# SmoothQuant woven further into the table lookups, and the softplus of the state-space scan in pairs of groups

## The chip, the core and the metric

The kernel runs on one core of one Trainium2 chip. The metric is the device time of one execution in microseconds. Three runs of the kernel before took 1949.47, 1953.06 and 1958.2 us; the median, 1953.06 us, is what the changed kernel is compared with.

## The reference, cut to what matters

The program is a stack of four residual blocks on x of shape (4 batches, 512 positions, 512 channels):

```python
x = x + smooth_quant_mlp(layernorm(x), fside, ctx)     # per batch; int8-like quantization
x = x + ghost_ffn(layernorm(x), lut, gate_idx, up_idx, down_idx)   # weights are lut[idx]
x = x + mamba(ctx, layernorm(x), ...)                  # state-space scan, gated by x
x = x + moe(layernorm(x), gate_w, w_gate, w_up, w_down)            # 32 experts, top 8
```

In the third block the step size goes through a softplus before the scan over the 512 positions, with 16 states for each of 512 inner channels:

```python
u  = silu(conv(in_proj(ctx)) + conv_b)
dt_low, Bm, Cm = split(x_proj(u))
dt = softplus(dt_proj(dt_low) + dt_b)
state = state * exp(dt * A) + (dt * u) * B;   y = sum_n(state * C)
```

`ctx` is an input, so everything up to `dt` and `dt * u` depends on no earlier block; only the gate with layernorm(x) does. The quantized multiplication scales both operands by column maxima, rounds each row to 127 steps of its own maximum, multiplies, and scales back.

## The kernel before, in words

The program is written as Python generators, each of which yields after a step. `weave` (L1053) takes several generators with a weight each and always advances the one that has done the smallest share of its weight. A scheduler then puts the emitted instructions into one queue for each engine; every engine works through its own queue in order. Pools hand out memory: when a pool is closed and another opened, the new tiles wait for the last use of what lay there.

**Lookups** (`lut_weights`, L317). The FFN's weights are built in 27 jobs of four steps. In a step VectorE compares the indices with a value (L335, `oh`, one-hot rows in bf16), TensorE multiplies them with the table in three bf16 parts (L341, `pw`), and ScalarE copies the result out (L350).

**SmoothQuant** (`smooth_quant`, L196; `quantize`, L159). One generator of 26 steps for each batch; `staggered` starts the next batch 15 steps after the one before. In `quantize` VectorE scales the rows (L166) and takes their maxima (L171 to L173), ScalarE rounds (L176, L180), TensorE transposes and ScalarE copies (L186, L187). It is called for x, for the weights w, for the intermediate a, and for the down weights `dw`. Outputs `o` are scaled on VectorE (L247) and added to x on GpSimd (L248). The four batches have 104 steps. In the kernel before, 40 of these are woven with the first 48 lookup steps, 48 with the rest (L1080 to L1082), and what is left with `prepare` of batch 0 (L1088).

**prepare** (L482), nine steps for each batch: for each of four groups of 128 channels a projection (`pi`), the convolution on VectorE (L496 to L505); then `px`, `xd`, and the softplus of each of the four groups (L519 to L537). The softplus is max(z, 0) + log(1 + exp(-|z|)), with the rounding of 1 + w put right by `lost`: Abs, Relu and Exp on ScalarE (L526 to L528), one operation on VectorE (L530), a subtraction on GpSimd (L531), Ln on ScalarE (L532), two additions and the product with u on GpSimd (L533 to L535), and the store of `dt` and `dt * u` to memory (`dts`, L536, through GpSimd's queue). Exp and Ln change the activation table (`ACT_TABLE_LOAD` in the profile). The tile `d` of a group has two buffers, `lost` has one.

**Scan** (`scan`, L539): 64 rounds for each batch. Each loads `d` from `dts` with its rows repeated for the 16 states (L557, SyncE's queue), takes exp on ScalarE (L562, `st`), the product with B on GpSimd (L564, `dBu`, three buffers), the scan itself on VectorE (L567 or L569) and the product with C (L570 on VectorE, L574 on GpSimd); TensorE sums the states (L580).

The scan of batch b is woven with the FFN of all batches in turn (`lut_ffn`, L353: layernorm L112, transposes `pt_x` L367 and copy `xT` L368, `pgu` L376 on TensorE, `g` and `h` L384 to L386, `po_f` L392), with `prepare` of batch b + 1, and with gate and routing of batch b - 1. `prepare` of batch 0 has no such company: it runs with the end of SmoothQuant. After the last batch come the experts (L921 to L976).

Of the kernel before, what the change touches and what calls it, by code (L numbers as in the profile page):

```python
# [16 lines left out]
F32 = mybir.dt.float32  # L17
# [4 lines left out]
AF = mybir.ActivationFunctionType  # L22
ALU = mybir.AluOpType
# [4 lines left out]
P = 128  # L28
NB = 4
S = 512  # L30
# [3 lines left out]
KH = HID // P  # L34
# [6 lines left out]
RANK = 16  # L41
# [19 lines left out]
class Kernel:  # L61
# [420 lines left out]
    def prepare(self, mp, up, b):  # L482

        nc, t = self.nc, self.t
        conv_b, dt_b, _ = (self.vecs[:, i, :] for i in range(3))
        cT = mp.tile([P, DC // P, S], F32, tag="c", name="cT", bufs=1)
        nc.sync.dma_start(out=cT, in_=t["ctxT"][b].rearrange("(k p) l -> p k l", p=P))
        u = self.u[b] = up.tile([P, KH, S], F32, tag="u", name="u", bufs=1)
        for e in range(KH):
            pi = self.bank(self.prep_tag, "pi")  # L490
            for k in range(DC // P):
                nc.tensor.matmul(
                    pi, lhsT=self.in_w[:, k, e * P : (e + 1) * P], rhs=cT[:, k, :], start=k == 0, stop=k == DC // P - 1
                )
            acc = mp.tile([P, S], F32, tag="acc", name="acc", bufs=1)
            nc.scalar.activation(  # L496
                acc, pi, AF.Identity, bias=conv_b[:, e : e + 1], scale=self.conv_w[:, e, 3:4]
            )
            for j in (2, 1, 0):
                a = 3 - j  # L500
                nc.vector.scalar_tensor_tensor(
                    acc[:, a:], pi[:, : S - a], self.conv_w[:, e, j : j + 1], acc[:, a:], ALU.mult, ALU.add
                )
            nc.scalar.activation(u[:, e, :], acc, AF.Tanh)
            nc.vector.scalar_tensor_tensor(u[:, e, :], u[:, e, :], 1.0, acc, ALU.add, ALU.mult)  # L505
            yield

        px = self.bank(self.prep_tag, "px")
        nx = RANK + 2 * NST
        for e in range(KH):  # L510
            nc.tensor.matmul(px[:nx, :], lhsT=self.xp_w[:, e, :], rhs=u[:, e, :], start=e == 0, stop=e == KH - 1)
        xd = mp.tile([P, DC // P, S], F32, tag="c", name="xd", bufs=1)[:nx, 0, :]
        nc.scalar.copy(xd, px[:nx, :])
        nc.scalar.dma_start(out=self.xdbl[b].rearrange("g n l -> (g n) l"), in_=xd)
        yield

        for e in range(KH):  # L519
            pd = self.bank(self.prep_tag, "pd")  # L520
            nc.tensor.matmul(
                pd, lhsT=self.dt_w[:, e * P : (e + 1) * P], rhs=xd[:RANK, :], start=True, stop=True
            )
            d = mp.tile([P, 2, S], F32, tag="dt", name="dt", bufs=2)
            dt, w = d[:, 0, :], d[:, 1, :]
            nc.scalar.activation(w, pd, AF.Abs, bias=dt_b[:, e : e + 1])  # L526
            nc.scalar.activation(dt, pd, AF.Relu, bias=dt_b[:, e : e + 1])
            nc.scalar.activation(w, w, AF.Exp, scale=-1.0)  # L528
            lost = mp.tile([P, S], F32, tag="acc", name="lost", bufs=1)
            nc.vector.tensor_scalar(lost, w, 1.0, -1.0, ALU.add, ALU.add)  # L530
            nc.gpsimd.tensor_tensor(lost, w, lost, ALU.subtract)  # L531
            nc.scalar.activation(w, w, AF.Ln, bias=1.0)  # L532
            nc.gpsimd.tensor_tensor(dt, dt, lost, ALU.add)  # L533
            nc.gpsimd.tensor_tensor(dt, dt, w, ALU.add)
            nc.gpsimd.tensor_tensor(w, dt, u[:, e, :], ALU.mult)  # L535
            nc.gpsimd.dma_start(out=self.dts[b, e * P : (e + 1) * P], in_=d)  # L536
            yield  # L537

    def scan(self, mp, b):  # L539

# [494 lines left out]
def run(steps):  # L1035
    for _ in steps:
        pass
# [25 lines left out]
@with_exitstack  # L1063
def tile_kernel(ctx: ExitStack, tc: tile.TileContext, t: dict):
    k = Kernel(tc, t)
    k.constants(ctx)
    scan = ExitStack()
    with ExitStack() as early:
        with ExitStack() as ffn:
            wp = ffn.enter_context(tc.tile_pool(name="wp", bufs=1, side="right"))  # L1070
            with ExitStack() as first:
                k.banks(first, t=2, m=2, y=2, d=2)
                ap = first.enter_context(tc.tile_pool(name="ap", bufs=2))
                sq = staggered([k.smooth_quant(ap, b) for b in range(NB)], 15)
                with ExitStack() as lut:
                    lc = lut.enter_context(tc.tile_pool(name="lc", bufs=1, side="right"))
                    lp = lut.enter_context(tc.tile_pool(name="lp", bufs=2, side="right"))
                    k.lut_tables(lc, wp)
                    lookups = k.lut_weights(lp, k.jobs)
                    weave((islice(sq, 40), 40), (islice(lookups, 48), 48))  # L1080
                    k.tile_rows(wp, lc)
                    weave((islice(sq, 48), 48), (lookups, 4 * len(k.jobs) - 48), (k.scratch(lc), 18))  # L1082

                pp = ffn.enter_context(tc.tile_pool(name="pp", bufs=1, side="right"))
                k.scan_weights(pp)
                k.prep_tag = "y"
                preps = 2 * KH + 1
                weave((k.prepare(pp, pp, 0), preps), (sq, 30 * NB - 88))  # L1088
            k.banks(early, t=2, m=2, y=1, d=3)
            k.prep_tag = "t"  # L1090
            bp = ffn.enter_context(tc.tile_pool(name="bp", bufs=2, side="right"))
            rp = ctx.enter_context(tc.tile_pool(name="rp", bufs=1))
            mp = scan.enter_context(tc.tile_pool(name="mp", bufs=2))
            k.routing_constants(rp)
            steps = (TPB // 2) * (NIC + 3)
            units = KH * 16
            routes = 2 * (TPB + 1)

            ffn_ = chain(*(k.lut_ffn(bp, b) for b in range(NB)))
            run(islice(ffn_, 4))  # L1100
            for b in range(NB):
                n = steps
                streams = [(k.scan(mp, b), units), (islice(ffn_, n), n)]
                if b + 1 < NB:
                    streams.append((k.prepare(pp, (pp, mp)[(b + 1) % 2], b + 1), preps))
                if b:
                    run(k.gate(mp, b - 1))
                    streams.append((k.route(rp, b - 1), routes))
                if b == NB - 1:
                    tok = k.slots(rp, k.tables[:1], 0, EARLY, ROOM[0], "a")  # L1110
                    at = k.slot_tokens(rp, tok, ROOM[0], "a")
                weave(*streams)
        ep = ctx.enter_context(tc.tile_pool(name="ep", bufs=2, side="right"))
        k.gu_tag = "m"
        full, nc = SLOTS // P, tc.nc
        two = [k.sums[j % 2] for j in range(full + 1)]
        first = k.pipeline(k.expert(ep, e, (k.xln[0], *at, 0), e, ROOM[0], two) for e in range(EARLY))
        weave((chain(k.gate(mp, NB - 1), k.route(rp, NB - 1)), KH + routes), (first, 2 * EARLY))
    scan.close()
    k.banks(ctx, t=4, g=4)  # L1120
    k.gu_tag = "g"
    tp = ctx.enter_context(tc.tile_pool(name="tp", bufs=6))
    at = k.slot_tokens(rp, k.slots(rp, k.tables, EARLY, NE, SLOTS, "u"), SLOTS, "u")
    at_b = k.slot_tokens(rp, k.slots(rp, k.tables[1:], 0, EARLY, ROOM[1], "b"), ROOM[1], "b")
    k.overflow(rp)
    calls = [(e, at, e - EARLY, SLOTS) for e in range(EARLY, NE)]
    for e in range(EARLY - LAST):
        calls.insert(2 * e + 1, (e, at_b, e, ROOM[1]))

    calls += [(e, at_b, e, ROOM[1]) for e in range(EARLY - LAST, EARLY)]  # L1130
    sums = [two] * (len(calls) - LAST) + [k.sums[2:] * 3] * LAST
    late = k.pipeline(
        k.expert(ep, e, (k.xln[1], *at, 0), col, n, s) for (e, at, col, n), s in zip(calls, sums)
    )
    run(islice(late, 2 * (len(calls) - LAST)))
    weave(
        (late, 2 * LAST),
        (
            chain(k.add_sums(tp, k.sums[:2], 0, NT // 2, True), k.add_sums(tp, k.sums[:2], NT // 2, NT, False)),
            NT // 2,  # L1140
        ),
    )
    run(k.add_sums(tp, k.sums[2:], NT // 2, NT, True))
    more = nc.values_load(k.more[0:1, 0:1], min_val=0, max_val=1)
    with tc.If(more):
        k.in_full(rp, ep, tp)
# [51 lines left out]
```

## Time and profile before

| | |
|---|---|
| median of three runs | 1953.06 us |
| the profiled execution | 1955.34 us |
| its span | 1953.5 us |
| granted TensorE clock, mean | 0.935 |
| TensorE busy | 1661.3 us (85%) |
| VectorE busy | 1196.9 us (61%) |
| GpSimd busy | 1001.9 us (51%) |
| ScalarE busy | 711.6 us (36%) |
| last lookup matmul | about 272.8 us |
| last addition of SmoothQuant (L248) | 340.4 us |
| first exponential of the scan (L562) | 350.7 us |
| first matmul of the FFN (L376) | 352.0 us |
| first expert gather (L902) | 1107.4 us |

How to read the profile: each line of the view in order of time has the start in us, the duration in us, the engine, the line of the kernel, the operation, output<-inputs by the program's names, the shape and the number of instructions merged into the line; in brackets stands how long the engine had been idle, and what it had waited for. PE is TensorE, PEld its weight loads, DVE is VectorE, ACT is ScalarE, POOL is GpSimd, SP is SyncE; a q behind the name is the engine's queue of DMA issues. The table of stretches has, for each stretch, the busy time of each engine in us with its number of instructions.

### The profile page before, as it was taken

Reading aid. Unit: us, or ns where it says so; the run is one execution under the profiler, and the core shown is the slowest. Engines: PE = TensorE matmul, PEld = TensorE weight load, DVE = VectorE, ACT = ScalarE, POOL = GpSimd, SP = SyncE. Lnnn points to the kernel's source line nnn. Section 1 sums busy time; section 2 is a strip of 40 time slices with the busy share of each in tenths; the row PEclk is TensorE's granted clock in tenths of the full one; section 3 lists DMA queues with packets and bytes.
Section 4 is the critical chain, followed back from the end, with each engine's and each line's share of the span. In section 5 each row is a group of like instructions: output and inputs, shape, how many; then the busy total and the mean of one; then the engine's idle time right before and its main releaser. Section 6 shows DMA issues by size and latency. Waiting matters only on the chain.

```text
span 1953.5 us, 25018 instructions
## 1 busy us (share of the span) xinstructions
PE 1661.3 (85%) x8836; PEld 983.6 (50%) x8845; DVE 1196.9 (61%) x2033; ACT 711.6 (36%) x1345; POOL 1001.9 (51%) x824
## 2 busy tenths in 40 slices
PE   4778875899889888898888588899999999999981
PEld 2444332656454545454545245455656656665640
DVE  6888864788799989998899734423222222232333
ACT  1554455545543554355333322222222222222210
POOL 3210113768755784578466642455555555555421
PEclk9989986899999898899899799999999999999995
DMA  9535611889887887778789696688887877778776
GB/s 264 142 104 165 203 60 35 224 200 226 213 236 162 200 218 201 172 195 207 192 209 221 175 226 140 152 195 177 184 181 157 178 180 169 164 166 191 148 163 210
DMA packets 190362, 351.94 MB, mean 180 GB/s; under 512 B 41826, under 2 KB 88258, under 8 KB 190228
## 3 DMA queue, kind: packets, MB, share of 16 engines
q1 hardware_dynamic: 147844, 253.00, 48.9%
q0 software_dynamic: 39952, 92.66, 24.0%
q10 hardware_dynamic: 2432, 4.59, 0.6%
q8 instruction: 72, 1.18, 0.3%
q14 instruction: 62, 0.51, 0.1%
HBM read 279.17 MB, written 79.47 MB: 184 GB/s over the span
## 4 chain that ended last, share of the span: by engine, by line
PE 35%; DMA 7%; DVE 5%; issue 2%; ACT 1%; POOL 1%; SPq 0%; ACTq 0%; POOLq 0%; DVEq 0%
PE pg L927 17%; PE po_e L956 8%; PE po_e L960 5%; PE pt_g L915 3%; DMA sums<-ey,to 2%; DMA xg<-xln,tokens 2%; DMA d<-dts 2%; DVE st L569 1%; DVE sc L570 1%; DMA acc<-sums 1%; POOL xg L902 0%; POOL dBu L564 0%; DVE lo_i L803 0%; PE pl L712 0%; DVE eh L945 0%
## 5 line engine op out<-in xcount | busy, mean ns | idle before, releaser
L970 POOL DMA_INDIRECT sums<-ey,to x168 | 261.3, 1555 | 314.1 <-DMA sums<-ey,to 129.8
L927 PE MATMUL pg<-exT,egu 128*128 128x320 f32 (+1 forms) x1536 | 402.7, 420 | 11.7 <-DVE exT L917 5.0
L564 POOL TENSOR_TENSOR dBu<-d,BC 128x512 f32<-128x512 f32 x256 | 333.9, 1315 | 107.8 <-DMA d<-dts 67.1
L927 PEld LDWEIGHTS pg<-exT,egu 128*128 128x128 f32 x1536 | 291.3, 192 | 126.4 <-issue 35.3
L569 DVE TENSOR_TENSOR_SCAN st<-st,dBu 128x512 f32<-128x512 f32 x192 | 230.8, 1216 | 32.1 <-POOL dBu L564 30.0
L562 ACT ACTIVATE st<-d,A 128x512 f32<-128x512 f32 x256 | 173.4, 689 | 202.1 <-DVE sc L570 125.8
L376 PE MATMUL pgu<-xT,wg 128*128 128x256 f32 (+1 forms) x704 | 189.4, 412 | 28.5 <-DVE h L386 23.5
L902 POOL DMA_INDIRECT xg<-xln,tokens x168 | 161.8, 963 | 90.5 <-PE pt_g L915 37.7
L944 DVE SCALAR_TENSOR_TENSOR eh<-eh,pg 64x128 f32<-64x128 f32 (+5 forms) x144 | 61.1, 425 | 223.5 <-ACT eh L943 222.4
L956 PE MATMUL po_e<-ed,eh 128*128 128x512 f32 (+1 forms) x336 | 171.5, 629 | 20.9 <-DVE eh L945 13.0
L376 PEld LDWEIGHTS pgu<-xT,wg 128*128 128x128 f32 (+1 forms) x704 | 133.5, 199 | 96.2 <-DVE h L386 34.6
L341 PE MATMUL pw<-oh,lut_t 128*32 128x344 bf16 (+1 forms) x2052 | 124.9, 356 | 65.6 <-DVE oh L335 65.3
L376 PE MATMUL pgu<-xT,wu 128*128 128x256 f32 (+1 forms) x704 | 176.8, 393 | 0.0
L969 ACT ACTIVATE ey<-po_e,gates 128x512 f32<-128x512 f32 (+1 forms) x104 | 68.7, 684 | 290.2 <-PE po_e L960 143.4
L967 DVE TENSOR_SCALAR ey<-po_e,gates 128x512 f32<-128x512 f32 x64 | 45.8, 747 | 201.3 <-PE po_e L960 201.3
L392 PE MATMUL po_f<-wd,h 128*128 128x512 f32 (+1 forms) x352 | 160.7, 613 | 2.9 <-DVE h L386 2.2
L376 PEld LDWEIGHTS pgu<-xT,wu 128*128 128x128 f32 (+1 forms) x704 | 136.2, 195 | 24.3 <-issue 3.0
L574 POOL TENSOR_TENSOR sc<-sc,BC 128x512 f32<-128x512 f32 x64 | 83.5, 1304 | 111.3 <-DVE sc L567 82.0
L570 DVE TENSOR_TENSOR sc<-st,BC 128x512 f32<-128x512 f32 x192 | 127.2, 678 | 17.9 <-PE py L580 17.3
L960 PE MATMUL po_e<-ed,eh 64*128 64x512 f32 (+1 forms) x336 | 112.8, 635 | 0.0
L341 PEld LDWEIGHTS <-lut_t 128*32 128x32 bf16 x2052 | 56.4, 101 | 111.9 <-issue 72.3
L392 PEld LDWEIGHTS po_f<-wd,h 128*128 128x128 f32 (+1 forms) x352 | 68.3, 197 | 87.3 <-issue 80.3
(259 smaller groups left out, 2194.1 us busy)
## 6 DMA issues: line engine op xcount, KB each, us to landing
d<-dts SPq DMA_DIRECT2D x256, 512.0 KB, 6.2
egu<-in_w_gate SPq DMA_DIRECT2D x40, 384.0 KB, 4.0
sums<-zero SPq DMA_DIRECT2D x16, 768.0 KB, 6.6
ix<-idx_b SPq DMA_DIRECT2D x16, 688.0 KB, 5.5
egu<-in_w_up SPq DMA_DIRECT2D x40, 256.0 KB, 5.6
ed<-in_w_down SPq DMA_DIRECT2D x40, 256.0 KB, 4.2
ed<-in_w_down SPq DMA_DIRECT2D x80, 128.0 KB, 4.3
acc<-sums SPq DMA_DIRECT2D x20, 512.0 KB, 9.1
```

What stands on the lines that cost most here:

```text
L341: nc.tensor.matmul(pt[i][32 * c : 32 * c + 32, :step], lhsT=self.lut_t[:, j, g, :], rhs=oh[:, c * n + i * step : c * n + (i + 1) * step], ...
L376: nc.tensor.matmul(pg[:m, j * W : (j + 1) * W], lhsT=w[:, k, c * P : c * P + m], rhs=xT[:, k, :], start=k == 0, stop=k == KH - 1,)
L392: nc.tensor.matmul(po, lhsT=h[:m, c, i * P : (i + 1) * P], rhs=self.wd[:m, c, :], start=c == 0, stop=c == NIC - 1,)
L562: nc.scalar.activation(st, d[:, 0, :], AF.Exp, scale=self.A[:, i : i + 1])
L564: product = nc.gpsimd.tensor_tensor(dBu, d[:, 1, :], BC[:, 0, :], ALU.mult)
L569: nc.vector.tensor_tensor_scan(st, st, dBu, 0.0, ALU.mult, ALU.add)
L570: nc.vector.tensor_tensor(sc, st, BC[:, 1, :], ALU.mult)
L902: nc.gpsimd.indirect_dma_start(out=xg[:m, :], out_offset=None, in_=xln, in_offset=bass.IndirectOffsetOnAxis(ap=tokens[:m, lo + j, col : co ...
L927: nc.tensor.matmul(pg[i][:, :hs], lhsT=w[:, k, i * P : (i + 1) * P], rhs=xT[:, k, z : z + hs], start=k == 0, stop=k == KH - 1,)
L956: nc.tensor.matmul(po[j][:m, :], lhsT=h[:, 0, b : b + m], rhs=wd[:, 0, :], start=True, stop=False)
L960: nc.tensor.matmul(po[j][:m, :], lhsT=h[r : r + R, 1, b : b + m], rhs=wd[r : r + R, 1, :], start=False, stop=True)
L970: nc.gpsimd.indirect_dma_start(out=sums[j], out_offset=bass.IndirectOffsetOnAxis(ap=to[:m, lo + j, col : col + 1], axis=0), in_=y[:m, :], ...
```

## The change

Two constants of the weave go up: 46 steps of SmoothQuant instead of 40 go with the first 48 lookup steps, 56 instead of 48 with the rest, so that 102 of the 104 steps are emitted beside the lookups and two beside `prepare` of batch 0. In `prepare` the softplus handles two groups at a time: the Abs and Relu of both, Exp of both, the `lost` part of both, Ln of both, then for each group the last addition, the product and the store. For batch 0 the subtraction, the additions and the product go to VectorE; for the other batches they stay on GpSimd. The buffers are as they were (two of `d`, one of `lost`). In the lines after it, the changed kernel's numbers are ten higher.

```diff
-        for e in range(KH):
-            pd = self.bank(self.prep_tag, "pd")
-            nc.tensor.matmul(
-                pd, lhsT=self.dt_w[:, e * P : (e + 1) * P], rhs=xd[:RANK, :], start=True, stop=True
-            )
-            d = mp.tile([P, 2, S], F32, tag="dt", name="dt", bufs=2)
-            dt, w = d[:, 0, :], d[:, 1, :]
-            nc.scalar.activation(w, pd, AF.Abs, bias=dt_b[:, e : e + 1])
-            nc.scalar.activation(dt, pd, AF.Relu, bias=dt_b[:, e : e + 1])
-            nc.scalar.activation(w, w, AF.Exp, scale=-1.0)
-            lost = mp.tile([P, S], F32, tag="acc", name="lost", bufs=1)
-            nc.vector.tensor_scalar(lost, w, 1.0, -1.0, ALU.add, ALU.add)
-            nc.gpsimd.tensor_tensor(lost, w, lost, ALU.subtract)
-            nc.scalar.activation(w, w, AF.Ln, bias=1.0)
-            nc.gpsimd.tensor_tensor(dt, dt, lost, ALU.add)
-            nc.gpsimd.tensor_tensor(dt, dt, w, ALU.add)
-            nc.gpsimd.tensor_tensor(w, dt, u[:, e, :], ALU.mult)
-            nc.gpsimd.dma_start(out=self.dts[b, e * P : (e + 1) * P], in_=d)
-            yield
+        tt = (nc.gpsimd if b else nc.vector).tensor_tensor
+        for e0 in range(0, KH, 2):
+            ds = []
+            for e in (e0, e0 + 1):
+                pd = self.bank(self.prep_tag, "pd")
+                nc.tensor.matmul(
+                    pd, lhsT=self.dt_w[:, e * P : (e + 1) * P], rhs=xd[:RANK, :], start=True, stop=True
+                )
+                d = mp.tile([P, 2, S], F32, tag="dt", name="dt", bufs=2)
+                nc.scalar.activation(d[:, 1, :], pd, AF.Abs, bias=dt_b[:, e : e + 1])
+                nc.scalar.activation(d[:, 0, :], pd, AF.Relu, bias=dt_b[:, e : e + 1])
+                ds.append(d)
+            for d in ds:
+                nc.scalar.activation(d[:, 1, :], d[:, 1, :], AF.Exp, scale=-1.0)
+            for d in ds:
+                dt, w = d[:, 0, :], d[:, 1, :]
+                lost = mp.tile([P, S], F32, tag="acc", name="lost", bufs=1)
+                nc.vector.tensor_scalar(lost, w, 1.0, -1.0, ALU.add, ALU.add)
+                tt(lost, w, lost, ALU.subtract)
+                tt(dt, dt, lost, ALU.add)
+            for d in ds:
+                nc.scalar.activation(d[:, 1, :], d[:, 1, :], AF.Ln, bias=1.0)
+            for e, d in zip((e0, e0 + 1), ds):
+                dt, w = d[:, 0, :], d[:, 1, :]
+                tt(dt, dt, w, ALU.add)
+                tt(w, dt, u[:, e, :], ALU.mult)
+                nc.gpsimd.dma_start(out=self.dts[b, e * P : (e + 1) * P], in_=d)
+                yield
...
-                    weave((islice(sq, 40), 40), (islice(lookups, 48), 48))
+                    weave((islice(sq, 46), 46), (islice(lookups, 48), 48))
                     k.tile_rows(wp, lc)
-                    weave((islice(sq, 48), 48), (lookups, 4 * len(k.jobs) - 48), (k.scratch(lc), 18))
+                    weave((islice(sq, 56), 56), (lookups, 4 * len(k.jobs) - 48), (k.scratch(lc), 18))
...
-                weave((k.prepare(pp, pp, 0), preps), (sq, 30 * NB - 88))
+                weave((k.prepare(pp, pp, 0), preps), (sq, 30 * NB - 102))
```

## The prediction

> **What bounds the kernel now.** I read the page first, then a table of stretches, then the order of time on each engine from 255 to 362 us, where both parts of the change meet. The page gives TensorE 85% of the span, but this is an average, so the table of stretches comes next (busy us and instructions per engine, then TensorE's clock, DMA share, GB/s):
>
> ```profile
> 0.00:273.00 273.00, 197.09 (x2599) 109.74 (x2607) 216.69 (x392) 118.18 (x187) 52.78 (x64) 0.94 0.54 164
> 273.00:341.00 68.00, 39.26 (x126) 17.57 (x127) 33.55 (x53) 38.20 (x57) 17.12 (x16) 0.71 0.13 42
> 352.00:1100.00 748.00, 658.68 (x3014) 402.12 (x3014) 666.23 (x1012) 335.47 (x545) 496.31 (x393) 0.94 0.82 203
> ```
>
> The lookups (0 to 273) are bound by VectorE: 216.7 of 273 us, and TensorE waits for its one-hot rows (65.3 us on the page's L341 row). The stretch 273 to 341 has no busy engine: nothing is over 58%. It is a chain of waits, the end of SmoothQuant's last batch woven with the first `prepare`. From 352 to 1100 (scan and FFN) VectorE is busy 89% and TensorE 88%; the experts after it are TensorE's. So a microsecond taken from the chain between 273 and 352 moves all later work forward, and one added to VectorE before 273 is paid in full.
>
> What ends that chain is seen in three answers. SyncE's queue, ScalarE, and TensorE with VectorE, in order of time:
>
> ```profile
> 340.44 0.37 SPq L622 DMA_DIRECT2D gate_w<-in_gate_w  x1
> 340.85 1.21 SPq L547 DMA_DIRECT2D BC<-xdbl  x2
> 342.17 16.35 SPq L557 DMA_DIRECT2D d<-dts  x7
> ```
> ```profile
> 340.45 0.81 ACT L112 ACTIVATE xn<-x,ln_off,ln_rs 128x512 f32<-128x512 f32 x1 [5.06 <-POOL x L248]
> ...
> 347.50 1.28 ACT L532 ACT_TABLE_LOAD   x1
> 348.80 0.63 ACT L532 ACTIVATE dt<-dt 128x512 f32<-128x512 f32 x1
> 349.45 1.28 ACT L562 ACT_TABLE_LOAD   x1
> 350.74 0.69 ACT L562 ACTIVATE st<-d,A 128x512 f32<-128x512 f32 x1
> ```
> ```profile
> 352.00 3.78 PE L376 MATMUL pgu<-xT,wg 128*128 128x256 f32 x8 [1.64 <-ACT xT L368]
> ```
> ```profile
> 352.01 1.22 DVE L567 TENSOR_TENSOR_SCAN sc<-st,dBu 128x512 f32<-128x512 f32 x1
> 356.79 2.45 DVE L569 TENSOR_TENSOR_SCAN st<-st,dBu 128x512 f32<-128x512 f32 x2 [3.56 <-POOL dBu L564]
> ```
>
> Everything new waits until 340.4, when GpSimd's last add of SmoothQuant (L248) frees the memory: the scan's loads (BC, d) and the FFN's `xn`. After that ScalarE still has two softplus groups with table loads before the first `st` at 350.74. VectorE's second scan waits to 356.8, because GpSimd is still at the fourth softplus.
>
> **SmoothQuant further beside the lookups.** The built order of the changed kernel shows what moves: ahead of the last one-hot row VectorE gets four instructions more, and only these, the scaling and row maximum of the last batch's weights (L166 2.29, L171 2.29, L172 0.17, L173 0.18: 4.9 us from their rows at 273.9 to 278.9). VectorE has little idle time there (1.96 us at 253.5 is the only long gap from 245 to 270), so the last one-hot row ends at 270.1 + 4.9 = 275.0. Bounds: 0 if gaps take them, 6 if earlier regrouping costs too; I take 4.9. The last lookup matmul follows 1.2 us later: 276.2, not 272.8 (before, its matmuls stood behind transposes; now these stand behind it). The load of `in_w` waits for it, so SyncE's seven small loads and `cT` (issued 272.9 to 276.3) move by 3.4 us and the first `pi` matmul from 280.5 to 284. Its cover: TensorE now has SmoothQuant's `q_w` transposes and `ph` to do in these 8 us; before it sat idle 6.65.
>
> SmoothQuant itself comes forward: the weights' row scale is known at about 273, not 278.9, so quantizing on ScalarE (2.93 + 2.00), transposes and copies bring the first `h` to 282.5 from 288.8. Behind it the order now favours SmoothQuant: all four `h` and the maximum of `a` stand ahead of the first convolution, and ScalarE has no softplus between `q_a`, `dw` and `q_d` (before: two Abs/Relu/Exp, one Ln, three loads at 1.28, 8.5 us, from 312.9 to 327), GpSimd none between its four adds. Walking the queues with the rows' durations: maximum of `a` 287.6, its scale 296.9, `q_a` 301, `dw` 307.5 to 311.4, `row_d` 317, four outputs with adds at 1.27 to 1.58: SmoothQuant ends at about 323, 17 us earlier. The walk has thirty hand-overs between engines, and a few tenths are easily missed in each: 323 to 330.
>
> `prepare` is not earlier: 3.5 us late at `pi`, four convolutions at 5.9 us each (from the starts of L496: 284.3, 290.3, 296.0, 302.0), `px`, `xd`: the first Abs at about 315 (312.9 before).
>
> **Softplus by pairs, batch 0.** Per pair ScalarE has four Abs/Relu (0.67), two Exp (0.63), two Ln (0.63) and two loads (1.28): 7.8 us, against 10.3 for two groups before. VectorE takes 16 operations off GpSimd (1.27 each): two-input fp32 rows of this shape on VectorE are L505, 0.69 us. So a group's sums cost 2.8 instead of 5.1 us. VectorE is idle enough here (33.6 of 68 us). The first pair: Abs 315, Exp of both by 321.5; then `xn` stands in ScalarE's queue and waits for SmoothQuant's end (323); Ln 325 to 326; VectorE's last product of group 0 at 327.7, store issued 327.7. That is where the first store was before (327.2): the pair's first store waits for its partner's work, and this eats what VectorE gains. What is late next is this store: it lands after 4.6 us (median of L536), at 332.3, now later than SmoothQuant's end, so `d` is issued at 332.3 instead of 342.2. The second pair uses the same two buffers, so its Abs waits for the landing: ScalarE 332.3 to 340.2 (Abs, Relu, Exp, Abs, Relu, Exp, load, Ln), load, first `st` at 341.5 (before 350.7); `xT`; then another Ln with two loads, second `st` at 346.8, second scan 347 to 348 (before 356.8). The FFN's second `xT` stands behind those loads: `pgu` at 347.7 (before 352.0). So the scan gains 9, the FFN 4. VectorE is the fuller of the two from there on, which puts the gain nearer the scan's: I take 8. Bounds: 2 (walk 7 us too fast) and 16 (the whole of SmoothQuant's lead).
>
> One rule speaks against VectorE's sums. The Trainium skill (SBUF — State Buffer, "Who interferes with whom") says that a VectorE operation with two SBUF inputs and a GpSimd operation that reads SBUF lock each other out, the second waiting for the first to end. The trace shows the like: L248 takes 1.26 us alone and 1.92 at most beside the lookups. By the row, the sums beside SmoothQuant's last adds cost some tenths; by the rule each of the two sums that meet an add loses up to 1.27 us, 2.5 in all, on the path to the first store. The start's gain would be 5.5 instead of 8. I keep 8, since by my walk only two of the four adds are left then.
>
> **Softplus by pairs, batches 1 to 3.** GpSimd keeps the sums, so each engine's work stays but for table loads. The built order has 14 loads here instead of 24, and 25 instead of 37 in all. The skill (ScalarE: Activation LUTs, "What ACT_TABLE_LOAD costs") gives 2.66 us for a switch with its drain; the trace shows the load alone, Relu ending 316.75, load 316.77, Exp 318.07. By the row 10 loads are 12.8 us of ScalarE, by the rule 26.6. Neither is on the path: ScalarE is busy 335 of 748 us, and VectorE waits for its `st` or `g` 11 us in the whole stage. I count 0 to 4 us gained.
>
> Against it stand GpSimd's blocks. In five of the six pairs the order has the second group's subtraction and addition (in two of the five only the addition), four sums and two stores in a row: up to 6 x 1.27 + 2 x 0.6 = 8.8 us, with the scan's products (L564) queued behind, and VectorE waits for these. Cover: three `dBu` buffers, each worth a scan step of 1.22 + 0.68: 5.7 us. Uncovered 8.8 + 1.3 - 5.7 = 4.4 us a block at most. Before, the groups were mixed with products, yet VectorE waited for L564 30.0 us in all, 22 times, among them 3.9 us at 528.6 where the fourth softplus (518 to 525) stood before the next scan; in the new order it is done well before that. I put blocks at 3 us lost and loads with cleared boundaries at 3 us gained: 0.
>
> **Sum.** The profiled execution took 1955.3 us (span 1953.5), 2.3 above the median. 1955.3 - 8 + 0 = 1947.3, and 2.3 less for the median: 1945.
>
> **Rivals.**
> 1. Both starts move with SmoothQuant's end, and the boundaries clear. For it: 340.4 gates both starts now. Against it: the first store's landing. Start -14, boundaries -5 (2.2 + 3.9 us wait at 518 to 529, less at the two others): 1934.
> 2. The lead is lost: the lookups' 4.9 us and the late store eat it. For it: `prepare` starts 3.5 us later and the first store is no earlier. Against it: ScalarE's queue ahead of `st` is shorter. It would be 1951.
> 3. Slower: GpSimd's blocks of 8.8 us stall the scan, 5 x 4.4 = 22 us on top of the waits now there. For it: GpSimd is 46 of 50 us busy at 450 to 500, where `prepare` runs; against it: there the waits are already part of the 30 us, and FFN work fills VectorE's queue. 1953 - 8 + 22 = 1967. It decides from 18 us, 3.6 a block, upward.
>
> **Chances.** The bound of 0.5%, about what a measurement can tell from no change, lies at 1943.3 and 1962.8. Likeliest case (1939 to 1949) 0.50, of which 0.20 falls below 1943.3; rival 1 0.20; rival 2 0.17; rival 3 0.13. Faster 0.40, same 0.47, slower 0.13. Range 1932 to 1962: it leaves out the best part of rival 1 and rival 3.
>
> **What would show it.** Last one-hot row near 275; last L248 near 323 to 330; first store near 328 and first `d` load right at its landing; first `st` near 341, `pgu` near 348; VectorE's wait for GpSimd's products near 30 us in 345 to 1100, with no wait over 4 us inside the pairs. A first `st` after 348, or that wait above 45 us, would make this wrong.

## The result, and the profile after

The changed kernel took 2000.1 us (median of four runs, 1995.8 to 2009.5) and the kernel before 1952.9 on the same chip: a ratio of 1.024, 95% interval 1.020 to 1.027. It is slower by 47 us, where I had forecast a gain of 8.

The profiled execution (2003.0 us, span 2001.2) is 47.7 us longer in span than that of before. Three marks cut it: the first exponential of the scan (351.3 us, 350.7 before), the first expert gather (1152.6, 1107.4 before) and the end. The start cost 0.6 us instead of bringing 8; the stage between the first two marks, called the scan stage below, went from 756.7 to 801.3, **44.6 us more**; after the gather it is 2.5.

The table of stretches of the changed kernel, to its own marks (busy us and instructions of TensorE, its weight loads, VectorE, ScalarE and GpSimd; TensorE's clock, DMA share, GB/s):

```profile
0.00:286.50 286.50, 204.88 (x2612) 112.05 (x2612) 219.88 (x396) 121.51 (x190) 50.28 (x64) 0.92 0.51 156
286.50:335.00 48.50, 31.55 (x120) 13.15 (x120) 26.97 (x47) 26.97 (x44) 6.46 (x7) 0.90 0.09 27
352.00:1145.00 793.00, 674.16 (x3020) 412.11 (x3020) 677.22 (x1019) 328.47 (x541) 489.03 (x392) 0.92 0.78 192
```

The lookups now end at 286.5, not 273: VectorE works 3.2 us longer there and idles 10.3 us longer. In the scan stage it has 11 us more of work in its stretch (some of it left-over softplus), in 45 us more of time. On VectorE both new losses are waits. TensorE's busy time in the scan stage rose too, by 15.5 us for six more matmuls, at a granted clock of 0.92 instead of 0.94; e15 below bears on whether that is the cause.

The start, in the order of time of SyncE's queue, ScalarE, TensorE and VectorE, answers line by line to the prediction's:

```profile
335.28 1.21 SPq L557 DMA_DIRECT2D BC<-xdbl  x2
...
343.11 15.74 SPq L567 DMA_DIRECT2D d<-dts  x7
```
```profile
334.80 0.81 ACT L112 ACTIVATE xn<-x,ln_off,ln_rs 128x512 f32<-128x512 f32 x1 [2.28 <-POOL x L248]
...
343.17 0.69 ACT L529 ACTIVATE dt<-pd,vecs 128x512 f32<-128x512 f32 x1 [5.10 <-DMA dts<-dt]
...
351.31 0.69 ACT L572 ACTIVATE st<-d,A 128x512 f32<-128x512 f32 x1
```
```profile
357.73 1.99 PE L376 MATMUL pgu<-xT,wg 128*128 128x256 f32 x8 [0.59 <-ACT xT L368]
```
```profile
353.55 1.21 DVE L577 TENSOR_TENSOR_SCAN sc<-st,dBu 128x512 f32<-128x512 f32 x1
...
355.19 3.01 DVE L544 TENSOR_TENSOR dt<-dt 128x512 f32<-128x512 f32 x1 [0.43 <-ACT dt L541]
358.12 1.22 DVE L579 TENSOR_TENSOR_SCAN st<-st,dBu 128x512 f32<-128x512 f32 x1
```

SmoothQuant's last addition now frees the memory at 334.8, 5.6 us earlier, and neither start gains by it: the `d` loads, which followed it at 342.2, now wait to 343.1 for the first store of the softplus. SmoothQuant is no longer what the start waits for; `prepare` is. The FFN's first matmul is 5.7 us later than before.

In the scan stage, VectorE's waits, before and after (what waited, for what: us in total, times, longest us):

```profile
DVE st L569 <- POOL dBu L564: 30.0, 22, 3.9
DVE sc L570 <- PE py L580: 17.3, 15, 2.6
...
DVE g L385 <- ACT g L384: 7.8, 6, 3.4
...
DVE st L569 <- ACT st L562: 1.5, 1, 1.5
```
```profile
DVE st L579 <- POOL dBu L574: 23.9, 21, 3.8
DVE sc L580 <- PE py L590: 20.4, 13, 7.1
DVE st L579 <- ACT st L572: 17.9, 7, 7.2
DVE g L385 <- ACT g L384: 16.2, 12, 4.0
DVE lost L537 <- POOL dt L539: 12.7, 6, 3.3
```

The wait for GpSimd's products, which I had watched, got smaller. Three others grew, by 37 us: for ScalarE's `st` and `g`, and a new one, `lost` of the second group, which waits until GpSimd has read `lost` of the first. One pair of batch 1 shows how they hang together, on ScalarE, GpSimd and VectorE:

```profile
466.16 1.16 ACT L533 ACTIVATE dt<-dt 128x512 f32<-128x512 f32 x2
...
471.23 0.63 ACT L541 ACTIVATE dt<-dt 128x512 f32<-128x512 f32 x1 [2.03 <-POOL lost L538]
475.49 0.63 ACT L541 ACTIVATE dt<-dt 128x512 f32<-128x512 f32 x1 [3.63 <-POOL lost L538]
...
489.03 0.69 ACT L529 ACTIVATE dt<-pd,vecs 128x512 f32<-128x512 f32 x1 [9.14 <-DMA dts<-dt]
```
```profile
474.19 1.26 POOL L538 TENSOR_TENSOR lost<-dt,lost 128x512 f32<-128x512 f32 x1 [0.43 <-DVE lost L537]
475.53 1.26 POOL L539 TENSOR_TENSOR dt<-dt,lost 128x512 f32<-128x512 f32 x1
476.75 2.49 POOL L544 TENSOR_TENSOR dt<-dt 128x512 f32<-128x512 f32 x2
479.21 2.49 POOL L545 TENSOR_TENSOR dt<-dt,u 128x512 f32<-128x512 f32 x2
481.64 1.15 POOL L546 DMA_DIRECT2D dts<-dt  x2
```
```profile
472.58 1.47 DVE L537 TENSOR_SCALAR lost<-dt 128x512 f32<-128x512 f32 x1 [3.35 <-POOL dt L539]
...
477.85 0.75 DVE L385 SCALAR_TENSOR_TENSOR g<-g,pgu 128x256 f32<-128x256 f32 x2 [3.20 <-ACT g L384]
...
490.98 2.35 DVE L579 TENSOR_TENSOR_SCAN st<-st,dBu 128x512 f32<-128x512 f32 x2 [7.16 <-ACT st L572]
```

Read it as a ring. GpSimd's sums of the first group end at 472.5; VectorE stood 3.35 us at the second `lost` until then; GpSimd subtracts it by 475.5; ScalarE, whose queue has both Ln in a row, stood for that with the FFN's `g` behind it; VectorE then stood for `g`. GpSimd's six sums and two stores last from 474.2 to 482.8. The second pair uses the same two `d` buffers, so its first Abs waits at the head of ScalarE's queue for the store to land, 9.14 us, with the scan's `st` behind, and VectorE stands 7.16. A wait of ScalarE for the landing occurs only this once in the scan stage; VectorE's wait for the second `lost` occurs six times, 12.7 us in all.

### The profile page after: what moved, and what is told of

The parts are those of the page before. It is cut to its first block, busy times and chain, and to the rows that moved or that the text cites. A ratio compares the mean times of both kernels' runs of the same rounds, so it can differ in the third digit from the quotient of the medians.

```text
span 2001.2 us, 25008 instructions
## 1 busy us (share of the span) xinstructions
PE 1675.6 (84%) x8845; PEld 988.6 (49%) x8845; DVE 1210.5 (60%) x2049; ACT 697.2 (35%) x1333; POOL 975.3 (49%) x808
## 5 line engine op out<-in xcount | busy, mean ns | idle before, releaser
L574 POOL TENSOR_TENSOR dBu<-d,BC 128x512 f32<-128x512 f32 x256 | 334.1, 1313 | 150.3 <-DMA d<-dts 83.3
L579 DVE TENSOR_TENSOR_SCAN st<-st,dBu 128x512 f32<-128x512 f32 x192 | 230.4, 1216 | 42.2 <-POOL dBu L574 23.9
L376 PE MATMUL pgu<-xT,wg 128*128 128x256 f32 (+1 forms) x704 | 192.5, 417 | 33.5 <-DVE h L386 27.9
L341 PE MATMUL pw<-oh,lut_t 128*32 128x344 bf16 (+1 forms) x2052 | 131.2, 370 | 71.9 <-DVE oh L335 71.6
L392 PE MATMUL po_f<-wd,h 128*128 128x512 f32 (+1 forms) x352 | 164.9, 626 | 7.9 <-DVE x L399 7.9
L584 POOL TENSOR_TENSOR sc<-sc,BC 128x512 f32<-128x512 f32 x64 | 83.2, 1300 | 120.0 <-DVE sc L577 86.4
L580 DVE TENSOR_TENSOR sc<-st,BC 128x512 f32<-128x512 f32 x192 | 127.8, 679 | 21.1 <-PE py L590 20.4
```

What stands on the lines that cost most here:

```text
L341: nc.tensor.matmul(pt[i][32 * c : 32 * c + 32, :step], lhsT=self.lut_t[:, j, g, :], rhs=oh[:, c * n + i * step : c * n + (i + 1) * step], ...
L376: nc.tensor.matmul(pg[:m, j * W : (j + 1) * W], lhsT=w[:, k, c * P : c * P + m], rhs=xT[:, k, :], start=k == 0, stop=k == KH - 1,)
L392: nc.tensor.matmul(po, lhsT=h[:m, c, i * P : (i + 1) * P], rhs=self.wd[:m, c, :], start=c == 0, stop=c == NIC - 1,)
L574: product = nc.gpsimd.tensor_tensor(dBu, d[:, 1, :], BC[:, 0, :], ALU.mult)
L579: nc.vector.tensor_tensor_scan(st, st, dBu, 0.0, ALU.mult, ALU.add)
L580: nc.vector.tensor_tensor(sc, st, BC[:, 1, :], ALU.mult)
```

## The experiments

Ratios are to the kernel before on the same chip; its medians in the four groups were 1955, 1963, 1957 and 1950 us, so ratios compare, not times. In brackets stands the 95% interval. One hundredth is 19.5 us. Marks such as the last lookup matmul or the scan stage are read from one profiled execution of each kernel. Theory A: the pairs of batches 1 to 3 cost the 47 us. Rival B: the weave does.

### The change in its parts (e1 to e4)

e1: the weave alone, old softplus.

```diff
-                    weave((islice(sq, 40), 40), (islice(lookups, 48), 48))
+                    weave((islice(sq, 46), 46), (islice(lookups, 48), 48))
...
-                    weave((islice(sq, 48), 48), (lookups, 4 * len(k.jobs) - 48), (k.scratch(lc), 18))
+                    weave((islice(sq, 56), 56), (lookups, 4 * len(k.jobs) - 48), (k.scratch(lc), 18))
```

> Only the two weave constants (and the rest count) are changed; the softplus is the old one, one group at a time. Theory A (the pairs of batches 1 to 3 cost the 47 us): within 8 us of 1953, and the stretch from the first scan to the first expert gather as long as before (about 757 us). Rival B (the weave costs it, through the lookups' 13.6 us and what they push back): 1990 or more.

Measured: 1.0084 (1.0052 to 1.0116). Last lookup matmul at 284.7 us, first exponential of the scan at 360.1.

e2: the paired softplus as in the change, weave 40, 48, 88 as before.

> The paired softplus in all four batches, the old weave constants. Theory A: 1992 to 2002, with the loss of some 45 us between the first scan and the first gather. Rival B: within 8 us of 1953.

Measured: 1.0171 (1.0112 to 1.0229); scan stage 789.9 us, first exponential at 350.4.

e3 and e4: pairs for batch 0, the old loop for the others; e3 with the new weave, e4 with the old one.

```diff
+        if b == 0:
+            tt = (nc.gpsimd if b else nc.vector).tensor_tensor
+            for e0 in range(0, KH, 2):
...
+            return
         for e in range(KH):
             pd = self.bank(self.prep_tag, "pd")
```

> New weave and pairs with VectorE's sums in batch 0; batches 1 to 3 have the old softplus, one group at a time with GpSimd's sums. Theory A: 1950 to 1962, so 40 us or more below the changed kernel. Rival B: 1990 or more.

Measured: 1.0053 (1.0027 to 1.0078); first exponential at 354.0, scan stage 760.4.

> Pairs with VectorE's sums in batch 0 alone; old weave, and old softplus in batches 1 to 3. Theory A: 1945 to 1955, since the start loses nothing to the lookups and batches 1 to 3 are untouched. Rival B says the same, 1945 to 1955. If it is over 1965, the loss comes from batch 0's pairs, and both fall.

Measured: 0.9969 (0.9953 to 0.9984); first exponential at 346.5, scan stage 759.8. Faster than both kernels.

So both A and B hold in part, and A's claim to the whole falls. From e4 to e2 the late pairs cost 0.020, from e3 to the changed kernel 0.018: 36 to 39 us (e2's interval alone is 11 us to either side). The weave costs 0.008 with the old softplus (e1) and with batch 0's pairs (e3 against e4): 16 us. The scan's first exponential shows only 9.4 and 7.5 us of that; the FFN's first matmul shows 15.2 (367.2 in e1, 352.0 before) and 11.5 (360.5 in e3, 349.0 in e4). Batch 0's pairs with VectorE's sums bring 0.003: 6 us.

### Which wait of the late pairs (e5, e6, e7, e9, e10, e15)

All of these have the old weave. e5: the first group's `lost` in the unused half of `xd`'s tile.

```diff
-        xd = mp.tile([P, DC // P, S], F32, tag="c", name="xd", bufs=1)[:nx, 0, :]
+        cx = mp.tile([P, DC // P, S], F32, tag="c", name="xd", bufs=1)
+        xd = cx[:nx, 0, :]
...
-            for d in ds:
+            for i, d in enumerate(ds):
...
-                lost = mp.tile([P, S], F32, tag="acc", name="lost", bufs=1)
+                lost = cx[:, 1, :] if i == 0 else mp.tile([P, S], F32, tag="acc", name="lost", bufs=1)
```

> Run of the pairs in all batches with the old weave (e2, 1988), where the first group's lost gets room of its own (the unused half of xd's tile), so that L537 of the second group needs not wait for GpSimd's L539 of the first. ScalarE's queue is in the same order. Theory A1 (that wait, 13.0 us of VectorE in e2, and the second Ln behind it): 1970 to 1978, and VectorE's wait for L539 gone. Rival A2 (the landing of the first pair's store) and rival A3 (ScalarE's long bursts themselves): 1983 to 1990.

Measured: 1.0103 (1.0071 to 1.0136), some 13 us below e2 by the ratios, as A1 said, and 9 by the scan stage of the profiles (781.1). The intervals of e2 and e5 overlap a little; e7 against e6 below, which differ in the same point, repeat the gain: 0.0070, and 11.6 us of the stage. The wait for L539 is gone, and VectorE's wait for the scan's products has grown from 27.9 us in e2 to 41.5.

e6: one more `yield` ahead of the second pair in batches 1 to 3, so ten steps in the weave. e7: e5 and e6 together.

> Run e2 with one empty step of prepare between the two pairs of batches 1 to 3 (ten steps instead of nine), so that the second pair stands 11 exponentials of the scan behind the first, not 3. Theory A2 (ScalarE stands at the second pair's Abs until the first pair's store has landed, 9.5 us): 1974 to 1980, and no Abs that waits for a DMA. A1: 1984 to 1990. A3: 1984 to 1990.

Measured: 1.0131 (1.0085 to 1.0176). No Abs waits for a landing any more, yet the scan stage took 789.4, no shorter than e2's 789.9, and the interval includes both claims. What the landing costs in the scan stage is not settled: the profile gives it next to nothing, the ratios 8 us. In e6's profile TensorE is busy 7 us longer than in e2's (679.0 against 671.8).

> Both together. A1 with A2: 1955 to 1968. A3 (neither wait is the cause; ScalarE's burst of some 9 us without a g or st is): over 1978.

Measured: 1.0061 (1.0030 to 1.0091); scan stage 777.8, still 18 us over e4. VectorE's waits in e7's scan stage (each run has its own line numbers; `st L582` is the changed kernel's L579):

```profile
DVE st L582 <- POOL dBu L577: 42.5, 30, 4.9
DVE g L385 <- ACT g L384: 17.6, 10, 5.8
...
DVE sc L580 <- POOL dBu L577: 6.6, 3, 4.9
```

With the `lost` wait gone, VectorE waits 49.1 us for the scan's products, which stand behind GpSimd's sums: 23 us more than in e4 (25.7), and for `g` 10 us more (7.1 in e4). This is my rival 3, which the changed kernel had hidden behind an earlier wait: from e2 to e5 to e7 the wait for the products goes from 27.9 to 41.5 to 49.1 us as the other waits are taken away.

e9 and e10 test that. Both leave out the correction by `lost` and the last addition in batches 1 to 3, e9 in pairs with the gap, e10 in single groups.

```diff
+                if b:
+                    continue
                 lost = mp.tile([P, S], F32, tag="acc", name="lost", bufs=1)
...
-                tt(dt, dt, w, ALU.add)
+                if b == 0:
+                    tt(dt, dt, w, ALU.add)
```

> Pairs in all batches with the gap of e6 and the old weave, but in batches 1 to 3 the softplus leaves out the correction by lost and the last addition (dt is then max(z, 0) alone): GpSimd has one product and one store for each group, 3.7 us in a row for a pair instead of 8.8, and Ln waits for no GpSimd. To be compared with e10, which leaves out the same in single groups. Theory A4 (what is left of the loss in e7, some 18 us against e4, are GpSimd's sums in a row and those who wait for them): within 6 us of e10. A3 (ScalarE's bursts): 12 us or more above e10.

Measured: 0.9937 (0.9906 to 0.9968), scan stage 755.0.

> e4 (pairs in batch 0 alone, old weave), with the correction by lost and the last addition left out in the single groups of batches 1 to 3, as in e9. GpSimd is rid of 36 operations of 1.27 us, 46 us, where VectorE waited 25.7 us for its products: 1935 to 1948 under every theory. It is the control for e9.

Measured: 0.9887 (0.9845 to 0.9928), scan stage 748.8. With short sums pairs lose 6.2 us of scan stage to single groups (medians: 6.1), and 9.8 us by the ratios, where e7 lost 18 to e4 by either. That is over A4's 6 and below A3's 12: one half to two thirds of the rest are GpSimd's sums and Ln's wait for them. The intervals of e9 and e10 overlap, so the last 6 to 10 us, perhaps ScalarE's bursts or the gap that only e9 has, are hardly more than the runs can tell.

e15: VectorE takes the sums in all batches.

```diff
-        tt = (nc.gpsimd if b else nc.vector).tensor_tensor
+        tt = nc.vector.tensor_tensor
```

> Pairs in all four batches, old weave, with VectorE taking the sums in all of them (e2 with one word changed). VectorE gets 48 operations of 0.69 us less the 16 of batch 0: 33 us if it is the bound all the time; it is rid of the waits for L539 (13) and for GpSimd's products (24 to 28). GpSimd's sums as the cause of what the pairs lose: ratio 1.000 to 1.010, below e2's 1.017, with no wait for L539. ScalarE's bursts and landings as the cause: 1.020 to 1.030.

Measured: 1.0054 (1.0030 to 1.0078), 23 us below e2. VectorE, busy 89% of the scan stage before, is given 25 us more of work (700.8 against 675.9 us busy) and the stage gets 19 us shorter (770.5). Its waits:

```profile
DVE st L579 <- POOL dBu L574: 19.3, 17, 3.9
...
DVE g L385 <- ACT g L384: 8.9, 11, 3.3
...
DVE st L579 <- ACT st L572: 3.3, 3, 1.5
```

In e2 these three were 24.0, 16.6 and 20.4 us, with 13.0 more for `lost`, which is gone. Every wait of the ring shrinks, though the pairs, their bursts and the shared buffers are as in e2. Giving VectorE the sums thus removes the ring's slow engine. TensorE's clock in the stage is 0.92 in e15 as in e2 (0.94 in e4), so these 19 us don't come from the clock. What it adds to the rest no run separates; e15 is still 0.0085, 17 us, above e4.

### Batch 0 (e8)

The old loop in single groups, with `nc.vector.tensor_tensor` in place of `nc.gpsimd.tensor_tensor` for batch 0.

> The kernel before with one change: in batch 0 VectorE takes the sums of the softplus, one group at a time; no pairs, old weave. If the gain of e4 (0.3%) comes from VectorE's sums: 1945 to 1951, first exponential of the scan at 344 to 347. If it comes from the pairs' fewer table loads: 1952 to 1956, at 350.

Measured: 0.9976 (0.9955 to 0.9997), first exponential at 346.0. As in e4 (0.9969, 346.5): the gain is VectorE's sums, and the pairs add nothing that can be told.

### The weave (e11 to e14)

Only the counts of e1's diff differ: 46, 48, 94 in e11; 40, 56, 96 in e12; 42, 46, 88 in e13; 40, 52, 92 in e14.

> The kernel before with the first weave constant alone (46 beside the first 48 lookup steps, then 48, then the rest). If the cost of the weave is VectorE work that comes ahead of the last one-hot row (my prediction's 4.9 us, which lies at the end): no change, 1953 to 1957 on the first chip's scale, ratio 1.000 to 1.002, last lookup matmul near 273. If it is SmoothQuant's chain standing in VectorE's queue wherever it is denser: ratio 1.003 to 1.006, last lookup matmul at 276 to 280.

Measured: 1.0097 (1.0068 to 1.0126), last lookup matmul at 285.0, first exponential at 361.6.

> The kernel before with the second weave constant alone (40, then 56, then the rest). If the cost is the work that comes ahead of the last one-hot row: most of e1's cost, ratio 1.006 to 1.010, last lookup matmul at 281 to 285. If it is spread with the density: ratio 1.003 to 1.006, last lookup matmul at 277 to 281.

Measured: 1.0088 (1.0058 to 1.0117), 283.9 and 358.5. Each constant alone costs as much as both. e12 lies where its first expectation put it; e11, which that theory had as free, fits neither. What e1, e11 and e12 share is that the scaling of the last weights stands ahead of the last one-hot rows. The next two leave it behind them.

> The kernel before with the weave 42 and 46: 88 steps as before, regrouped between the one-hot rows, with the scaling of the last batch's weights behind the last one-hot row as before. If the cost of the new weave comes from the four instructions ahead of the last one-hot rows: ratio 0.998 to 1.002, last lookup matmul at 272 to 276. If it comes from the regrouping: ratio 1.004 to 1.009, last lookup matmul at 279 to 285.

Measured: 0.9991 (0.9971 to 1.0010), 274.8 and 352.9. Regrouping alone costs nothing.

> The kernel before with the weave 40 and 52: 92 steps, of which the scaling of the last batch's weights still stands behind the last one-hot row. Four instructions as the cause: ratio 0.998 to 1.002, last lookup matmul at 272 to 277. Regrouping as the cause: ratio 1.004 to 1.009, last lookup matmul at 279 to 285.

Measured: 1.0063 (1.0042 to 1.0084), 275.0 and 355.9. The lookups say "the four instructions", the time says that there is a second cost. ScalarE in e14 shows it:

```profile
321.25 0.67 ACT L526 ACTIVATE dt<-pd,vecs 128x512 f32<-128x512 f32 x1
...
341.65 0.69 ACT L526 ACTIVATE dt<-pd,vecs 128x512 f32<-128x512 f32 x1 [2.63 <-DMA dts<-dt]
...
352.81 0.69 ACT L526 ACTIVATE dt<-pd,vecs 128x512 f32<-128x512 f32 x1 [5.48 <-DMA dts<-dt]
```

With SmoothQuant put first, `prepare` reaches its first Abs at 321.3 (312.9 before), and then the third and fourth group each wait for the landing of an earlier store, with `st` behind. SmoothQuant ends 2.2 us earlier (338.2), the scan starts 5 us later, and the FFN 11 (362.9). So e14 loses 0.0063 where e1 loses 0.0084, with its lookups on time: late one-hot rows are not the whole cost of the weave. How the changed kernel's share divides between the two is not shown.

Over all runs, the last lookup matmul starts at 272.4 to 279.1 us in the twelve kernels with the scaling behind the last one-hot row and at 283.9 to 286.0 in the five that have it ahead (the changed kernel, e1, e3, e11, e12). The kernel before has the earliest of the twelve; the means of the two sets, 275 and 285, lie 10 us apart. With the four instructions, work of other engines in the same steps moves too, so what is shown is the place of these steps, not of the four alone. VectorE in the changed kernel:

```profile
272.12 0.75 DVE L335 TENSOR_SCALAR oh<-ix,lut_v 128x2048 bf16<-128x2048 bf16 x1 [0.91 <-PE pw L341]
273.40 0.75 DVE L335 TENSOR_SCALAR oh<-ix,lut_v 128x2048 bf16<-128x2048 bf16 x1 [0.53 <-PE pw L341]
275.89 0.75 DVE L335 TENSOR_SCALAR oh<-ix,lut_v 128x2048 bf16<-128x2048 bf16 x1 [1.74 <-PE pw L341]
277.63 2.29 DVE L166 TENSOR_TENSOR w<-w,pt_col_w 128x2048 f32<-128x2048 f32 x1 [0.99 <-PE pt_col_w L150]
...
280.50 2.28 DVE L171 TENSOR_REDUCE sc_w<-w 128x4 f32<-128x2048 f32 x1
```

The scaling takes its 4.9 us as forecast, at 277.6 (273.9 before): not earlier but later, since its own input comes later. Around it VectorE stands for `pw` and `pt_col_w`, 4.4 us with the 0.24 of a later row, and one-hot rows that used to be done by then still follow. Where the rest of the 10.3 us of idle time lies is not shown.

## Why the prediction was wrong, point by point

**The last one-hot row: the first failed term.** I counted VectorE's added work (4.9 us) and no added waits: last lookup matmul +3.4. It was +13.6 in the profiles, of which VectorE's busy time gave 3.2 and its idle time 10.3; over all runs about +10, since the profile of before is the earliest of its kind. "VectorE has little idle time there" was true of the kernel before; the moved steps brought their own waits into the queue.

**The walk behind it was right, 10 to 12 us late.** Forecast and measured: first `pi` 284 and 296.1; first `h` 282.5 and 293.4; first Abs 315 and 326.7; first store 327.7 and 339.8; `d` 332.3 and 343.1; first `st` 341.5 and 351.3; second `st` 346.8 and 356.5; `pgu` 347.7 and 357.7. In this profile the one mis-sized term carries through: its excess is 10.2 us, and the start gain forecast as 8 came out as a loss of 0.6. For the start, then, rival 2 was right: the lookups and the late store ate the lead. One sum of the walk was off by itself: from the second pair's Abs to the end of its Ln I had 7.9 us, the instructions that I listed make 5.9, or 7.1 with the table load of Exp that I left out, and it took 6.8.

**SmoothQuant's end: 323 to 330 forecast, 334.8 measured.** The same offset. But the premise, that 340.4 gates both starts, failed once the order changed: in e14 SmoothQuant ended earlier and the scan began later, because `prepare` had been put behind it. I had the mechanism in my own walk (the first store's landing) and yet took earlier SmoothQuant for gain.

**VectorE's sums in batch 0: right.** From e1 to e3 the first exponential moves from 360.1 to 354.0; e8 shows the gain without pairs, so the table loads saved there were worth nothing that can be told.

**Batches 1 to 3, "blocks 3 lost, loads 3 gained: 0": the second failed step, and the larger.** They cost 36 to 39 us. I did look for GpSimd's sums in a row, and put their price on the scan's products, in waits for L564. I did not ask what the pair does with one `lost` buffer: the second L537 stands in VectorE's queue until GpSimd has read the first, and e5, which parts the two, gains 9 to 13 us. e15, which takes the sums off GpSimd and that wait with them, gains 19 to 23. Nor did I price ScalarE's queue: two Ln in a row behind GpSimd, with `g` and `st` behind them. "Neither is on the path: ScalarE is busy 335 of 748 us" was the mistake: a queue that is half idle is on the path when its head waits.

**The test that I named was half right.** A first `st` after 348 was seen (351.3). The other sign, VectorE's wait for GpSimd's products above 45 us, was not (27.0), and still rival 3 named the culprit: in e7, with the `lost` wait gone, that wait is 49.1. Rival 3's 22 us for it compares with e7's 18 over e4. Its price was too low because the same sums were waited for at two more places.

**The table loads.** They fell as counted, from 37 to 25 in all and from 24 to 14 in batches 1 to 3, and the scan stage got longer. What they alone are worth there no run shows.

**The sharing of VectorE and GpSimd.** I weighed the rule of the Trainium skill (SBUF — State Buffer, "Who interferes with whom") only for the sums beside SmoothQuant's additions. There it cost little, as the rows had it: L537 took 0.81 us and L538 1.10 where they take 0.43 and 0.69 with GpSimd idle (346.41 and 346.87). It bit 20 us later: the L544 that begins at 355.19 took 3.01 us instead of 0.69 while GpSimd ran L584 and L574, 1.26 us each, and the second scan stood behind it, to 358.1 where I had 347 to 348. One such stretch is 2.3 us.

What stays open: how the landing of a store is worth 9 us of ScalarE's wait and hardly anything in the stage (e6), the last 6 to 10 us of the pairs (e9 against e10), how the weave's 16 us divide between the late one-hot rows and the order of `prepare` behind SmoothQuant (e14), and what TensorE's lower clock adds.

## What to carry to other kernels

When work is batched in twos, list each buffer that has one copy and each queue that now holds two waiting instructions in a row; the price is what stands behind them in the in-order queues of all engines, not the busy time of any. When steps are moved into a stage bound by one engine, they bring their waits as well as their work: look whether they end up ahead of the bound's last instructions, and whether what they wait for is there by then. And a wait that shrinks in the profile does not acquit the engine waited for, since an earlier wait for the same engine can hide it (e5, e7).

## What the runs showed of the hardware that was not expected

A one-input VectorE operation was stretched as well as a two-input one: L537 takes 0.43 us with GpSimd idle (346.41) and took 1.47 at 472.58, while GpSimd's product of 1.26 us ran from 472.51; it ended 0.3 us after that product. The L537 at 348.39 did the same: 1.30 us, ending 0.3 us after the product that ran from 347.77 to 349.41.
